# Softplus remainders summed by TensorE, and two products with their weights held: an attention and selective-scan block on one core

## The chip, the core and the metric

The kernel runs on one core of a Trainium2 chip. The engines named below are TensorE (PE; its weight loads are listed as PEld), VectorE (DVE), ScalarE (ACT), GpSimd (POOL) and SyncE (SP, which issues the DMAs). Each engine works through its own queue in order; they meet through semaphores. The metric is the device time of one execution in microseconds, as the median over several runs.

## What is computed

The input x has shape (16, 256, 32, 32): 16 batch items of 256 channels by 1024 positions. Two layers follow each other. The first is a group norm with an attention block (4 heads of 32) and a feed-forward part. The second is a group norm with a selective scan. Cut to what the change touches:

```python
ctx = sigmoid(conv(xp, gate_w) + gate_b)              # gate: 3 taps, 256 -> 256 channels
u, z = split(xs @ in_proj_w.T)                        # 512 + 512 channels
u = silu(causal depthwise conv(u))
dt, Bm, Cm = split(u @ x_proj_w.T)
delta = softplus(dt @ dt_proj_w.T + dt_proj_b)        # 512 channels x 1024 positions
A = -exp(A_log)                                       # 512 x 64
# for each position, with a state of 64 values per channel
h = exp(delta * A) * h + (delta * u) * B_t
y = sum over the 64 states of h * C_t
y = (y + u * D) * silu(z)
x = x + (y @ out_proj_w.T * ctx).reshape(B, C, H, W)  # a reshape, not a transpose
```

The last line reads a (1024 positions, 256 channels) matrix as (256, 1024) without turning it. Output channel c, position l is therefore token 4c + l // 256, channel l % 256.

## The kernel before

**The scan sets the frame.** Per batch item there are 512 channels x 64 states = 32,768 rows of 1024 positions, cut into 256 *units* of 128 rows. For unit n the main loop does, in this order:

- `load(n + 6)`: a DMA spreads two rows of delta * u (DRAM tensor `dus`) over 128 partitions into one of seven `dub` buffers; for every eighth unit a further load brings `pieces`, the rows of delta.
- `inputs(n + 4)`: POOL multiplies `dub` by B (line 956).
- one step of `outputs`: PE multiplies finished states by C into `yb` (line 998) and, once in eight units, turns the sum (line 1010); ACT copies the results out.
- `scan(n)`: DVE runs the recurrence over 128x1024 (line 973).
- `decay(n + 2)`: PE rebuilds delta from three bfloat16 pieces and spreads it over the states (line 965, into `a`), and ACT takes Exp with A as a scale per partition (line 967). There are two `a` buffers, so the matmuls for unit n + 2 wait until scan n has read its own.

All arithmetic queues keep the order in which the program was written: a chain of dependencies at the end of the kernel fixes it. The DMAs on SP are ordered by the framework's scheduler.

**Side work is a generator.** While batch item b is scanned, the kernel prepares item b + 1 (`first_norm`, `attention_layer`, `scan_inputs`) and finishes item b - 1 (`gate_and_store`). Each `yield` hands back a share of a unit, and after each unit the loop takes the next step when it is due:

```python
if at >= (1 if b + 1 < B else 8):
    due -= 1.0
    while due <= 0.0:
        due += gap(next(side, 1e9), rate)
```

A step with a share of 1 or more is never followed by another in the same unit, and `rate` stretches the shares so that all steps fit into 247 of the 256 units. A longer list of steps moves all others closer together. Item 0 is prepared alone before the first scan, and item 15 is finished alone after the last one.

**Softplus** stands at the end of `scan_inputs`. For each of the four blocks of 128 channels (`d`) and each half of 512 positions (`hf`) it computes softplus as relu(v) + log(1 + e) with e = exp(-|v|), corrected by what rounding s = 1 + e lost. Matmul (800), Abs (802), Exp (803), s (808), Relu into PSUM (809), two DVE operations for relu and the correction (813, 814), Ln (828), a DVE difference (832). Delta is then cut into three bfloat16 pieces: ACT casts (833, 842), and DVE subtracts each piece from what is left in PSUM (841, 845, the second straight into the third piece). DVE multiplies by u (837). Both halves of a block go through the steps together, about seven steps a block. PSUM tiles come from a pool of two (`mm`).

**Gate** (`gate`, line 730). The positions are the stationary operand, every fourth of them, and the weights stream through, so that the result comes out as the reshape needs it: tokens on partitions, channels along the free axis. 12 matmuls of 128x256 for each tile of 512 and two one-row matmuls for the bias (736), then Tanh (739).

**Output product** (`gate_and_store`, line 910). It has the same form: 128 tokens, every fourth, are the stationary operand, four matmuls of 128x256 are one step, eight steps make the item. Two DVE operations a tile (897, 899) multiply by the gate and add the residual, one tile behind PE.

Of the kernel before, what the change touches and what calls it, by code (L numbers as in the profile page):

```python
# [11 lines left out]
F32 = mybir.dt.float32  # L12
BF16 = mybir.dt.bfloat16
AF = mybir.ActivationFunctionType
ALU = mybir.AluOpType
# [4 lines left out]
P = 128  # L20
C = 256
KC = C // P
L = 1024
HL = 512
# [5 lines left out]
ND = DI // P  # L30
# [20 lines left out]
def attention_then_scan_kernel(  # L51
# [86 lines left out]
    def col(name, i=0, n=1):  # L138
        o, w = _COLS[name]
        assert i + n <= w  # L140
        return vec[:, o + i : o + i + n]

    gate_b = const.tile([1, C], F32, name="gate_b")
    nc.sync.dma_start(gate_b, gate_bias)
    one_row = const.tile([1, P], F32, name="one_row")
    nc.vector.memset(one_row, 1.0)
    ident = const.tile([P, P], F32, name="ident")
    make_identity(nc, ident)
    avg = const.tile([P, P], F32, name="avg")
    nc.vector.memset(avg, 1.0 / C)  # L150
    eps = const.tile([P, 1], F32, name="eps")
# [485 lines left out]
    def scan_inputs(b):  # L637
# [81 lines left out]

        gates = {}  # L720

        def gate(o, hf, q, k):
            if (hf, q, k) == (0, 0, 0):
                gates["g"] = work("g")
            if (q, k) == (0, 0):
                gates["ps"] = psum("g_ps")
            g, ps = gates["g"], gates["ps"]
            first = o * HL + hf * 2 + q
            for t in range(3):
                nc.tensor.matmul(  # L730
                    ps[:, ts(q, C)], xp[k][:, ds(first + t, P, 4)], wg_s[:, k, t, :],
                    start=(k == 0 and t == 0), stop=False,
                )
            if k < KC - 1:
                return
            nc.tensor.matmul(ps[:, ts(q, C)], one_row, gate_b, start=False, stop=True)
            if q == 1:
                table("tanh")
                nc.scalar.activation(g[:, hs(hf)], ps, AF.Tanh, scale=0.5)
                if hf == 1:  # L740
                    nc.sync.dma_start(gs[ts(o, P), :], g)

# [5 lines left out]
        for d in range(ND):  # L748
            for t in range(2):
                tap(d, t)  # L750
                if d + 1 < ND:
                    project(d + 1, t)
                yield 1
            tap(d, 2)
            table("tanh")
            nc.scalar.activation(ups[d][:, :L], us[d], AF.Tanh)
            gate(d // 2, d % 2, 0, 0)
            yield 1
            gate(d // 2, d % 2, 0, 1)
            yield 1.5  # L760
            nc.vector.scalar_tensor_tensor(us[d], ups[d][:, :L], 1.0, us[d], ALU.add, ALU.mult)
            ups[d] = None
            nc.sync.dma_start(ud[ts(d, P), :], us[d])
            gate(d // 2, d % 2, 1, 0)
            yield 1
            gate(d // 2, d % 2, 1, 1)
            yield 1.5
        gates.clear()
        del xp, body
# [25 lines left out]
        dus = dram.tile([DI, L], F32, name="dus", tag="dus")  # L795
        dpv = dps.rearrange("(k q e p x) t -> k p e q x t", k=ND, q=4, e=2, p=3)

        def begin(d, hf):
            ps = psum("d_ps")
            nc.tensor.matmul(ps, wdt4[:, ts(d, P)], dt[:, hs(hf)], start=True, stop=True)  # L800
            e = hwork("sp_e")
            nc.scalar.activation(e, ps, AF.Abs, bias=col("dt_b", d))
            nc.scalar.activation(e, e, AF.Exp, scale=-1.0)
            return ps, e

        def more(d, ps, e):
            s = hwork("sp_s")
            nc.scalar.activation(s, e, AF.Copy, bias=1.0)
            nc.scalar.activation(ps, ps, AF.Relu, bias=col("dt_b", d))
            return ps, e, s  # L810

        def rest(ps, e, s):
            nc.vector.scalar_tensor_tensor(ps, s, 1.0, ps, ALU.subtract, ALU.subtract)
            nc.vector.tensor_tensor(ps, ps, e, ALU.subtract)

        table("log")
        items = [begin(0, 0)]
        yield 1
        for d in range(ND):
            items = [more(d, *items[0]), begin(d, 1)]  # L820
            yield 1.3
            items[1] = more(d, *items[1])
            rest(*items[0])
            yield 1.1
            rest(*items[1])
            for ps, e, s in items:
                table("log")
                nc.scalar.activation(s, s, AF.Ln)
            yield 1.3
            pc = [ptp.tile([P, L], BF16, name="pc", tag="pt") for _ in range(3)]  # L830
            for hf, (ps, e, s) in enumerate(items):
                nc.vector.tensor_tensor(ps, s, ps, ALU.subtract)
                nc.scalar.copy(pc[0][:, hs(hf)], ps)
            yield 1.1
            du = work("du")
            for hf, (ps, e, s) in enumerate(items):
                nc.vector.tensor_tensor(du[:, hs(hf)], us[d][:, hs(hf)], ps, ALU.mult)
            nc.sync.dma_start(dus[ts(d, P), :], du)
            yield 1.1
            for hf, (ps, e, s) in enumerate(items):  # L840
                nc.vector.tensor_tensor(ps, ps, pc[0][:, hs(hf)], ALU.subtract)
                nc.scalar.copy(pc[1][:, hs(hf)], ps)
            yield 1.1
            for hf, (ps, e, s) in enumerate(items):
                nc.vector.tensor_tensor(pc[2][:, hs(hf)], ps, pc[1][:, hs(hf)], ALU.subtract)
            items, ps, e, s = [], None, None, None
            for p in range(3):
                for e in range(2):
                    nc.sync.dma_start(dpv[d, p, e], pc[p][e:P:2])
            if d + 1 < ND:  # L850
                items = [begin(d + 1, 0)]
            yield 1.1
        st.update(zs=zs, gs=gs, ud=ud, rows=rows, dps=dps, dus=dus)
        st["ys"] = dram.tile([DI, L], F32, name="ys", tag="ys")
        yield 1
# [18 lines left out]
    def gate_and_store(b):  # L874
        if "gate" not in state[b]:
            for go in gate_loads(b):
                go()
        ys, us, zs, gs, xs, wo_s, come = state[b].pop("gate")
        for d in range(ND):
            come.pop(0)()  # L880
            nc.vector.scalar_tensor_tensor(us[d], us[d], col("D", d), ys[d], ALU.mult, ALU.add)
            ys[d] = None
            yield 0.6
            come.pop(0)()
            nc.gpsimd.tensor_tensor(us[d], us[d], zs[d], ALU.mult)  # L885
# [7 lines left out]
        ready = []  # L893

        def finish():
            for o, hf, ps in ready:
                nc.vector.scalar_tensor_tensor(ps, gs[o][:, hs(hf)], 1.0, ps, ALU.add, ALU.mult)
# [4 lines left out]
            ready.clear()  # L902

        for o in range(KC):
            for hf in range(2):
                ps = psum3("m_ps")
                for q in range(2):
                    first = o * HL + hf * 2 + q
                    for d in range(ND):
                        nc.tensor.matmul(  # L910
                            ps[:, ts(q, C)], us[d][:, ds(first, P, 4)], wo_s[:, d, :],
                            start=(d == 0), stop=(d == ND - 1),
                        )
                    if q == 1:
                        finish()
                    if come:
                        come.pop(0)()
                    yield 1.3
                ready.append((o, hf, ps))
        finish()  # L920
        del ps
        yield 1
        state[b].clear()

# [245 lines left out]
```

## Time and profile before

| | |
|---|---|
| runs | 12599.05, 12651.92, 12653.68 us; median 12651.92 |
| the profiled execution | 12609.3 us, span 12607.5 us |
| granted TensorE clock over the span, share of full | 0.799 |
| first scan starts, last scan ends | 426.1 us, 12560.8 us |
| batch items 0 to 14 | 762 to 778 us each |
| batch item 15, with no next item to prepare | 608 us |
| DMA | 2820 MB, mean 224 GB/s |
| chain of waits, by engine | DVE 37%, PE 32%, issue 13%, ACT 8%, DMA 7%, POOL 3% |

The span is cut into the time before the first scan (item 0 is prepared), sixteen stretches of 256 units, and 47 us after the last scan. Times of single instructions below come from the one profiled execution. A group's row reads: line, engine, operation, output<-inputs, shapes, count, then busy us in total, mean ns of one, the idle time of the engine just before them, and what ended it. A float32 matmul stands in the trace as two passes, so its count is twice that of the program.

### The profile page before, as it was taken

How to read it: one execution, taken by the hardware profiler on the slowest of the kernel's cores; microseconds unless marked ns; L12 is line 12 of the kernel's file. 1: busy time of each engine (PE TensorE's matmuls, PEld its weight loads, DVE VectorE, ACT ScalarE, POOL GpSimd, SP SyncE). 2: the span in 40 equal slices, each digit the busy share in tenths (PEclk: the TensorE clock that was granted, in tenths of full speed). 3: DMA queues.
4: the chain of work that ended last, by engine and by line, in shares of the span. 5: the costliest groups of instructions: out<-in, count | busy, mean ns of one | idle time of the engine just before them, and what ended most of it. 6: DMA issues, size and time to landing. Idle time of an engine off the chain costs nothing.

```text
span 12607.5 us, 421113 instructions
## 1 busy us (share of the span) xinstructions
PE 9517.2 (75%) x184752; PEld 5493.8 (44%) x184752; DVE 11264.3 (89%) x7482; ACT 7523.0 (60%) x10758; POOL 10030.6 (80%) x4201
## 2 busy tenths in 40 slices
PE   6676876868778687786878768687686877868777
PEld 2344444444444444444444444444444444444445
DVE  2799999899999899898998999999999998989998
ACT  3565655656656565565656656565565665656554
POOL 0587878878788787887878878788887878878798
PEclk7887977878878697887878878797787978878755
DMA  1566667676676766767666676766767667676676
GB/s 53 178 224 239 220 214 239 221 244 219 216 238 227 245 216 223 240 219 245 226 223 235 220 240 221 241 219 222 237 224 247 217 223 241 221 245 217 230 250 231
DMA packets 1070137, 2819.91 MB, mean 224 GB/s; under 512 B 324162, under 2 KB 402243, under 8 KB 1068292
## 3 DMA queue, kind: packets, MB, share of 16 engines
q1 hardware_dynamic: 1068292, 2792.97, 65.0%
q8 instruction: 1444, 23.66, 0.8%
q14 instruction: 401, 3.28, 0.1%
HBM read 2513.82 MB, written 261.62 MB: 220 GB/s over the span
## 4 chain that ended last, share of the span: by engine, by line
DVE 37%; PE 32%; issue 13%; ACT 8%; DMA 7%; POOL 3%; SPq 1%; DVEq 0%; POOLq 0%; ACTq 0%
DVE h L973 27%; PE yb L998 6%; PE a L965 5%; ACT a L967 4%; DMA dub<-dus 3%; PE av L531 3%; POOL dub L956 3%; PE st_ps L543 3%; DVE over L449 2%; PE z_ps L680 2%; PE s_ps L469 2%; PE g_ps L730 2%; PE yb L1010 1%; PE m_ps L910 1%; DVE u L716 1%
## 5 line engine op out<-in xcount | busy, mean ns | idle before, releaser
L956 POOL TENSOR_TENSOR dub<-dub,bt 128x1024 f32<-128x1024 f32 x4096 | 9805.4, 2420 | 2446.0 <-DMA dub<-dus 2241.7
L973 DVE TENSOR_TENSOR_SCAN h<-a,dub 128x1024 f32<-128x1024 f32 x4096 | 9176.7, 2275 | 705.4 <-ACT a L967 406.0
L967 ACT ACTIVATE a<-a,acol 128x1024 f32<-128x1024 f32 x4096 | 4464.1, 1090 | 3157.7 <-PE a L965 3092.6
L965 PE MATMUL a<-pieces,pick 48*128 48x512 bf16 x8192 | 1914.0, 458 | 2473.6 <-DVE h L973 2362.0
L998 PEld LDWEIGHTS yb<-h,cd 128*32 128x32 f32 x131072 | 2496.9, 128 | 2639.8 <-issue 1332.2
L998 PE MATMUL yb<-h,cd 128*32 128x64 f32 x131072 | 3266.9, 252 | 342.4 <-ACT y L1004 234.8
L965 PEld LDWEIGHTS <-pick 48*128 48x128 bf16 x8192 | 597.0, 95 | 2886.7 <-issue 2256.4
L1004 ACT COPY y<-yb 128x256 f32<-128x256 f32 x2048 | 763.3, 373 | 598.5 <-PE yb L998 589.1
L531 PE MATMUL av<-pt,vv 128*64 128x512 f32 x2048 | 607.7, 674 | 2.9 <-ACT sums L520 1.6
L551 ACT ACTIVATE pt<-st_ps 128x512 f32<-128x512 f32 x1024 | 552.9, 597 | 82.9 <-PE st_ps L543 82.0
L1010 PE MATMUL yb<-turn,y 128*32 128x16 f32 x32768 | 590.1, 214 | 2.3 <-issue 1.2
L543 PE MATMUL st_ps<-sp 33*128 33x512 f32 x2048 | 583.2, 646 | 2.9 <-ACT pt L551 2.9
L1010 PEld LDWEIGHTS yb<-turn,y 128*32 128x32 f32 x32768 | 571.7, 159 | 2.6 <-ACT y L1004 1.4
L730 PE MATMUL g_ps<-w,xp 128*128 128x256 f32 x1464 | 457.0, 452 | 0.1
L1014 ACT COPY yo<-yb 128x128 f32<-128x128 f32 x512 | 135.3, 264 | 519.1 <-PE yb L1010 510.9
L730 PEld LDWEIGHTS g_ps<-w,xp 128*128 128x128 f32 x1464 | 368.7, 326 | 67.7 <-issue 58.7
L469 PE MATMUL s_ps<-kd,qm 64*128 64x512 f32 x1022 | 367.5, 617 | 14.0 <-DVE kd L444 7.5
L449 DVE CUSTOM_DVE_ANT_0 over<-s_ps,over 128x512 f32<-128x512 f32 x512 | 326.8, 676 | 24.4 <-PE s_ps L469 24.4
L910 PE MATMUL m_ps<-w,xs 128*128 128x256 f32 x1024 | 321.6, 464 | 11.4 <-POOL xs L885 11.4
L716 DVE SCALAR_TENSOR_TENSOR u<-up,cwh,u 128x1024 f32<-128x1024 f32 x192 | 302.7, 1576 | 27.9 <-ACT u L708 27.7
L477 ACT ACTIVATE over<-s_ps 128x512 f32<-128x512 f32 x511 | 275.3, 595 | 32.8 <-PE s_ps L469 32.8
L910 PEld LDWEIGHTS m_ps<-w,xs 128*128 128x128 f32 x1024 | 262.9, 328 | 59.3 <-issue 26.7
(180 smaller groups left out, 7126.8 us busy)
## 6 DMA issues: line engine op xcount, KB each, us to landing
dub<-dus SPq DMA_DIRECT2D x4096, 512.0 KB
dps<-pc SPq DMA_DIRECT2D x384, 128.0 KB
pieces<-dps SPq DMA_DIRECT2D x1024, 48.0 KB
xs<-in_x_dram SPq DMA_DIRECT2D x64, 512.0 KB
xs<-kept SPq DMA_DIRECT2D x64, 512.0 KB
zs<-z SPq DMA_DIRECT2D x64, 512.0 KB
ud<-u SPq DMA_DIRECT2D x64, 512.0 KB
dus<-du SPq DMA_DIRECT2D x64, 512.0 KB
```

What stands on the lines that cost most here:

```text
L469: nc.tensor.matmul(s, qm[c // NJ][r, c % NJ], keys[r], start=True, stop=True)
L531: nc.tensor.matmul(av[ts(e, 2 * DH)], vv[j // (NJ // 2)][:, j % (NJ // 2), 2 * pair + e, :], pts[e], start=(j == 0), stop=(j == NJ - 1),)
L543: nc.tensor.matmul(s, ka[r, ts(j, P)], qa[r, hs(hf)], start=True, stop=True)
L730: nc.tensor.matmul(ps[:, ts(q, C)], xp[k][:, ds(first + t, P, 4)], wg_s[:, k, t, :], start=(k == 0 and t == 0), stop=False,)
L910: nc.tensor.matmul(ps[:, ts(q, C)], us[d][:, ds(first, P, 4)], wo_s[:, d, :], start=(d == 0), stop=(d == ND - 1),)
L956: nc.gpsimd.tensor_tensor(v, v, blocks[units[n][0]]["bt"], ALU.mult)
L965: nc.tensor.matmul(a[:, hs(hf)], w, pieces[r], start=True, stop=True)
L967: nc.scalar.activation(a, a, AF.Exp, scale=acol[:, at : at + 1])
L973: nc.vector.tensor_tensor_scan(now["h", e][:, i, :], decays.pop(n), loaded.pop(n), 0.0, ALU.mult, ALU.add)
L998: nc.tensor.matmul(yb[ts(g, 32), ts(s, 64)], cd[:, at // 16, ts(c, 32)], hbuf[:, :, at : at + 8], start=(c == 0), stop=(c == 1),)
L1004: nc.scalar.copy(y2[:, r], yb[:, :256])
L1010: nc.tensor.matmul(some[ts(r, 32), x], y2[:, r, x:256:8], turn[:, x], start=True, stop=True)
```

## The change

Softplus becomes a generator for one half tile, with two halves in flight four steps apart:

- The relu stays in PSUM, and PE adds to it there: identity times Ln(s), and minus-identity times the correction. The correction itself is one DVE operation on SBUF tiles.
- s = e + 1 is made by POOL.
- After each bfloat16 piece PE subtracts it in PSUM with a bfloat16 minus-identity; all three pieces are casts by ACT.
- PSUM tiles come from a cycle of three banks.
- 36 steps of one unit each take the place of 29 steps with shares of 1 to 1.3. The same six piece DMAs and one `dus` DMA a block are issued as their pieces are done.

The gate holds its weights stationary and streams 512 positions, so that six matmuls make one tile, with channels on partitions; the bias moves into the Tanh. The output product holds its weights as well (four matmuls of 128x512 a step), DVE joins it with the gate into an SBUF tile, and PE turns each tile back with four matmuls of 128x128 against the identity, reading every fourth column. Three small constants are added.

```diff
+    less = const.tile([P, P], F32, name="less")
+    nc.vector.tensor_scalar(less, ident, -1.0, None, ALU.mult)
+    less_b = const.tile([P, P], BF16, name="less_b")
+    nc.vector.tensor_copy(less_b, less)
...
-            for t in range(3):
+            for at in ((0, 1), (2,), (3, 4), (5,))[part]:
+                k, t = divmod(at, 3)
                 nc.tensor.matmul(
-                    ps[:, ts(q, C)], xp[k][:, ds(first + t, P, 4)], wg_s[:, k, t, :],
-                    start=(k == 0 and t == 0), stop=False,
+                    ps, wg_s[:, k, t, ts(o, P)], xp[k][:, ds(hf * HL + t, HL)],
+                    start=(at == 0), stop=(at == 5),
                 )
-            nc.tensor.matmul(ps[:, ts(q, C)], one_row, gate_b, start=False, stop=True)
...
-        def rest(ps, e, s):
-            nc.vector.scalar_tensor_tensor(ps, s, 1.0, ps, ALU.subtract, ALU.subtract)
-            nc.vector.tensor_tensor(ps, ps, e, ALU.subtract)
...
+        def softplus(d, hf):
+            at = hs(hf)
+            ps = psum3("d_ps")
+            nc.tensor.matmul(ps, wdt4[:, ts(d, P)], dt[:, at], start=True, stop=True)
+            e = hwork("sp_e")
+            table("log")
+            nc.scalar.activation(e, ps, AF.Abs, bias=col("dt_b", d))
+            yield
+            nc.scalar.activation(e, e, AF.Exp, scale=-1.0)
+            yield
+            s = hwork("sp_s")
+            nc.gpsimd.tensor_scalar(s, e, 1.0, None, ALU.add)
+            nc.scalar.activation(ps, ps, AF.Relu, bias=col("dt_b", d))
+            yield
+            nc.vector.scalar_tensor_tensor(e, s, 1.0, e, ALU.subtract, ALU.subtract)
+            table("log")
+            nc.scalar.activation(s, s, AF.Ln)
+            yield
+            nc.tensor.matmul(ps, ident, s, start=False, stop=False, skip_group_check=True)
+            nc.tensor.matmul(ps, less, e, start=False, stop=True, skip_group_check=True)
+            del s, e
+            yield
...
+            nc.vector.tensor_tensor(du[:, at], us[d][:, at], ps, ALU.mult)
+            for p in range(3):
+                if p > 0:
+                    yield
+                    nc.tensor.matmul(
+                        ps, less_b, pc[p - 1][:, at], start=False, stop=True, skip_group_check=True
+                    )
+                nc.scalar.copy(pc[p][:, at], ps)
...
+        going = []
         for d in range(ND):
...
+            for hf in range(2):
+                going.append(softplus(d, hf))
+                for _ in range(4):
+                    for g in going:
+                        next(g)
+                    yield 1
+                if len(going) == 2:
+                    del going[0]
...
+        def project(o, k):
+            ps = psum3("m_ps")
+            for d in range(ND):
+                nc.tensor.matmul(
+                    ps, wo_s[:, d, ts(k, P)], us[d][:, hs(o)],
+                    start=(d == 0), stop=(d == ND - 1),
+                )
+            return ps
+
+        def join(o, k, ps):
+            v = gated[o, k] = hwork("v")
+            nc.vector.scalar_tensor_tensor(v, gs[k][:, hs(o)], 1.0, ps, ALU.add, ALU.mult)
+
+        def turn_back(o, hf):
+            ps = psum3("o_t")
+            for q in range(2):
+                for k in range(KC):
+                    nc.tensor.matmul(
+                        ps[:, ds(q * C + k * P, P)], gated[o, k][:, ds(hf * 2 + q, P, 4)], ident,
+                        start=True, stop=True,
+                    )
+            turned.append((o, hf, ps))
+
+        work_on = [("p", 0, 0), ("p", 0, 1), ("p", 1, 0), ("t", 0, 0), ("p", 1, 1), ("t", 0, 1), ("t", 1, 0), ("t", 1, 1)]
```

In a middle batch item the program's own order puts the eight output steps on units 17 to 24 (before: 17 to 23 and 25), attention on 78 to 126 (before: 79 to 130), the gate on 178 to 201 (184 to 207) and softplus on 209 to 244 (215 to 243).

More of the change, by code (lines that the diff above doesn't have):

```diff
@@ L141, in col @@
         return vec[:, o + i : o + i + n]
[L143 to L146, printed above, removed]
+    gate_b = const.tile([P, KC], F32, name="gate_b")
+    nc.sync.dma_start(gate_b, gate_bias.rearrange("o (k p) -> p (o k)", p=P))
+    nc.vector.tensor_scalar(gate_b, gate_b, 0.5, None, ALU.mult)
     ident = const.tile([P, P], F32, name="ident")
     make_identity(nc, ident)
+    less = const.tile([P, P], F32, name="less")
+    nc.vector.tensor_scalar(less, ident, -1.0, None, ALU.mult)
+    less_b = const.tile([P, P], BF16, name="less_b")
+    nc.vector.tensor_copy(less_b, less)
     avg = const.tile([P, P], F32, name="avg")
@@ L720, in scan_inputs, with gate @@
         gates = {}
-        def gate(o, hf, q, k):
-            if (hf, q, k) == (0, 0, 0):
+        def gate(o, hf, part):
+            if (hf, part) == (0, 0):
                 gates["g"] = work("g")
-            if (q, k) == (0, 0):
+            if part == 0:
                 gates["ps"] = psum("g_ps")
             g, ps = gates["g"], gates["ps"]
-            first = o * HL + hf * 2 + q
-            for t in range(3):
+            for at in ((0, 1), (2,), (3, 4), (5,))[part]:
+                k, t = divmod(at, 3)
                 nc.tensor.matmul(
-                    ps[:, ts(q, C)], xp[k][:, ds(first + t, P, 4)], wg_s[:, k, t, :],
-                    start=(k == 0 and t == 0), stop=False,
-                )
-            if k < KC - 1:
-                return
-            nc.tensor.matmul(ps[:, ts(q, C)], one_row, gate_b, start=False, stop=True)
-            if q == 1:
-                table("tanh")
-                nc.scalar.activation(g[:, hs(hf)], ps, AF.Tanh, scale=0.5)
+                    ps, wg_s[:, k, t, ts(o, P)], xp[k][:, ds(hf * HL + t, HL)],
+                    start=(at == 0), stop=(at == 5),
+                )
+            if part == 3:
+                nc.scalar.activation(
+                    g[:, hs(hf)], ps, AF.Tanh, scale=0.5, bias=gate_b[:, o : o + 1]
+                )
                 if hf == 1:
@@ L756, in scan_inputs @@
             nc.scalar.activation(ups[d][:, :L], us[d], AF.Tanh)
-            gate(d // 2, d % 2, 0, 0)
+            gate(d // 2, d % 2, 0)
             yield 1
-            gate(d // 2, d % 2, 0, 1)
+            gate(d // 2, d % 2, 1)
             yield 1.5
@@ L763, in scan_inputs @@
             nc.sync.dma_start(ud[ts(d, P), :], us[d])
-            gate(d // 2, d % 2, 1, 0)
+            gate(d // 2, d % 2, 2)
             yield 1
-            gate(d // 2, d % 2, 1, 1)
+            gate(d // 2, d % 2, 3)
             yield 1.5
@@ L796, in scan_inputs @@
         dpv = dps.rearrange("(k q e p x) t -> k p e q x t", k=ND, q=4, e=2, p=3)
-        def begin(d, hf):
-            ps = psum("d_ps")
-            nc.tensor.matmul(ps, wdt4[:, ts(d, P)], dt[:, hs(hf)], start=True, stop=True)
+        dus_of, parts = {}, {}
+        def softplus(d, hf):
+            at = hs(hf)
+            ps = psum3("d_ps")
+            nc.tensor.matmul(ps, wdt4[:, ts(d, P)], dt[:, at], start=True, stop=True)
             e = hwork("sp_e")
+            table("log")
             nc.scalar.activation(e, ps, AF.Abs, bias=col("dt_b", d))
+            yield
@@ L803, in begin @@
             nc.scalar.activation(e, e, AF.Exp, scale=-1.0)
-            return ps, e
-        def more(d, ps, e):
+            yield
             s = hwork("sp_s")
-            nc.scalar.activation(s, e, AF.Copy, bias=1.0)
+            nc.gpsimd.tensor_scalar(s, e, 1.0, None, ALU.add)
             nc.scalar.activation(ps, ps, AF.Relu, bias=col("dt_b", d))
-            return ps, e, s
-        def rest(ps, e, s):
-            nc.vector.scalar_tensor_tensor(ps, s, 1.0, ps, ALU.subtract, ALU.subtract)
-            nc.vector.tensor_tensor(ps, ps, e, ALU.subtract)
@@ L816, in scan_inputs @@
-        table("log")
-        items = [begin(0, 0)]
-        yield 1
-        for d in range(ND):
[L820 to L852, printed above, removed]
@@ new lines, in softplus @@
+            yield
[7 more added lines that the diff above has]
+            yield
+            if hf == 0:
+                dus_of[d] = work("du")
+                parts[d] = [ptp.tile([P, L], BF16, name="pc", tag="pt") for _ in range(3)]
@@ new lines, in softplus @@
+            du, pc = dus_of[d], parts[d]
+            nc.vector.tensor_tensor(du[:, at], us[d][:, at], ps, ALU.mult)
[6 more added lines that the diff above has]
+                nc.scalar.copy(pc[p][:, at], ps)
+                if hf == 1:
+                    if p == 0:
+                        nc.sync.dma_start(dus[ts(d, P), :], dus_of.pop(d))
+                    for e in range(2):
+                        nc.sync.dma_start(dpv[d, p, e], pc[p][e:P:2])
@@ new lines, in softplus @@
+            if hf == 1:
+                del parts[d]
+            yield
+        going = []
+        for d in range(ND):
+            for hf in range(2):
[6 more added lines that the diff above has]
+                    del going[0]
+        for _ in range(4):
+            next(going[0])
+            yield 1
+        going.clear()
@@ L892, in gate_and_store @@
             come += fetches(state[b + 2].setdefault("tok", []), state[b + 2]["kept"])
-        ready = []
+        turned, gated = [], {}
         def finish():
-            for o, hf, ps in ready:
-                nc.vector.scalar_tensor_tensor(ps, gs[o][:, hs(hf)], 1.0, ps, ALU.add, ALU.mult)
+            for o, hf, ps in turned:
                 t = xs[o][:, hs(hf)]
@@ L901, in finish @@
                     nc.sync.dma_start(out[b, ts(o, P), :], xs[o])
[L902 to L919, printed above, removed]
+            turned.clear()
+        def project(o, k):
[16 more added lines that the diff above has]
+                        start=True, stop=True,
+                    )
+            turned.append((o, hf, ps))
+        work_on = [("p", 0, 0), ("p", 0, 1), ("p", 1, 0), ("t", 0, 0), ("p", 1, 1), ("t", 0, 1), ("t", 1, 0), ("t", 1, 1)]
+        joined = []
+        for what, o, i in work_on:
+            for j in joined:
+                join(*j)
+            joined.clear()
+            finish()
+            if what == "p":
+                joined.append((o, i, project(o, i)))
+            else:
+                turn_back(o, i)
+            if come:
+                come.pop(0)()
+            yield 1.3
         finish()
-        del ps
         yield 1
```

## The prediction

> **What bounds the kernel now.** I read the page's engine totals first, then its costliest groups, then busy time by stage, then single rows.
>
> ```profile
> PE 9517.2 (75%) x184752; PEld 5493.8 (44%) x184752; DVE 11264.3 (89%) x7482; ACT 7523.0 (60%) x10758; POOL 10030.6 (80%) x4201
> ...
> L956 POOL TENSOR_TENSOR dub<-dub,bt 128x1024 f32<-128x1024 f32 x4096 | 9805.4, 2420 | 2446.0 <-DMA dub<-dus 2241.7
> L973 DVE TENSOR_TENSOR_SCAN h<-a,dub 128x1024 f32<-128x1024 f32 x4096 | 9176.7, 2275 | 705.4 <-ACT a L967 406.0
> L967 ACT ACTIVATE a<-a,acol 128x1024 f32<-128x1024 f32 x4096 | 4464.1, 1090 | 3157.7 <-PE a L965 3092.6
> ```
>
> VectorE (DVE) is busy 89%; 9177 of its 11264 us are the 4096 scans, and side work is squeezed between them. It idles only 12607.5 - 11264.3 = 1343 us. What takes an instruction off DVE therefore pays nearly in full, unless another engine then makes a scan wait. The last batch has no side preparation and shows the next floor: 608 us, POOL busy 600.
>
> Batch 4 (start 3512.8 us, 762.6 us long) by stage: output product, attention, z product, u and gate, dt/B/C product, softplus, and ten units with no side work. Columns: length, busy us (instructions) of PE, PEld, DVE, ACT, POOL, then granted clock, DMA share, GB/s.
>
> ```profile
> 3577.70:3612.60 34.90, 30.13 (x468) 23.60 (x467) 29.45 (x20) 12.54 (x16) 29.52 (x13) 0.90 0.76 269
> 3756.10:3888.00 131.90, 119.45 (x2549) 58.23 (x2548) 120.62 (x55) 107.36 (x165) 123.96 (x54) 0.99 0.70 241
> 4009.80:4038.60 28.80, 28.31 (x405) 13.26 (x405) 24.89 (x19) 17.78 (x24) 21.68 (x11) 0.89 0.67 218
> 4038.60:4125.00 86.40, 74.63 (x1244) 50.01 (x1243) 84.70 (x49) 49.07 (x67) 76.74 (x29) 0.96 0.61 211
> 4125.00:4144.20 19.20, 17.95 (x306) 9.66 (x305) 15.54 (x8) 10.87 (x15) 13.85 (x7) 0.91 0.63 210
> 4144.20:4245.70 101.50, 60.43 (x1353) 35.30 (x1356) 95.80 (x80) 70.27 (x108) 72.37 (x32) 0.66 0.69 227
> 4245.70:4267.60 21.90, 16.38 (x391) 10.77 (x382) 21.88 (x11) 12.37 (x16) 13.92 (x6) 0.50 0.60 204
> ```
>
> Length less DVE busy is what DVE lost: 5.5 us in the output product, 11.3 in attention, 1.7 in the gate stage, 5.7 in softplus. So softplus is DVE's stage and PE is spare there, at a clock of 0.66; in the output product and attention PE is as full as DVE. A bare unit costs 21.9/10 = 2.19 us.
>
> **The change, part by part.** *Softplus, DVE.* These rows are what each half tile costs now:
>
> ```profile
> L813 DVE SCALAR_TENSOR_TENSOR d_ps<-sp_s,d_ps 128x512 f32<-128x512 f32 x127 | 87.4, 688 | 59.5 <-ACT d_ps L809 59.4
> L814 DVE TENSOR_TENSOR d_ps<-d_ps,sp_e 128x512 f32<-128x512 f32 x127 | 88.8, 699 | 4.4
> L832 DVE TENSOR_TENSOR d_ps<-sp_s,d_ps 128x512 f32<-128x512 f32 x127 | 80.7, 680 | 0.8 <-ACT pc L833 0.7
> L841 DVE TENSOR_TENSOR d_ps<-d_ps,pc 128x512 f32<-128x512 f32 x127 | 81.0, 683 | 0.7 <-ACT pc L842 0.7
> L845 DVE TENSOR_TENSOR pc<-d_ps,pc 128x512 bf16<-128x512 f32 x127 | 80.2, 672 | 1.5 <-DMA dps<-pc 0.8 <-ACT pc L842 0.7
> L800 PE MATMUL d_ps<-dt,wdt 128*128 128x512 f32 x254 | 202.3, 892 | 32.9 <-DVE pc L845 21.2 <-ACT d_ps L809 11.7
> ```
>
> All five DVE operations go (0.688+0.699+0.680+0.683+0.672 = 3.42 us); the product with u stays. One comes: (s-1)-e with every operand in SBUF. No such row of this size exists: the same operation reading PSUM takes 0.668 (L670), and half of the 128x1024 SBUF rows 0.79 (L716) to 0.98 (L881). I take 0.79, the in-place one. Net 2.63 us a half, 8 halves: 21.1 us a batch, 316 us over the 15 batches that run beside scans.
>
> *Softplus, what the other queues get.* Per half PE gains identity times s and minus-identity times e (float32, two passes each) and two bfloat16 products; ACT swaps the copy L808 (0.628) for a third cast (0.591); POOL gains s = e + 1. For that I bound 0.44 (an eighth of the 128x4096 memset, 3.51) to 1.18 (half of L956), taking 0.9. DMAs are the same in number and still trail the scans' loads, six units ahead. The steps now come one per unit, four units per half: 36 units against 30, the rest of the batch moving some six units earlier.
>
> In steady state four units need DVE 4 x 2.19 + 0.79 + 0.67 = 10.2 us; POOL 4 x 2.36 + 0.9 = 10.3; ACT 4 x 1.09 + 0.9 of y copies + seven operations of 4.4 = 9.7. Nothing is left spare, so waits decide. The worst unit holds the finish of one half and the start of the next: six float32 passes in a row on PE. Behind them in PE's queue stand the y products of the scan output (0.65 to 1.1) and the decay matmuls (0.4 to 0.6), then ACT's Exp of 1.09, for which a scan waits, since only two decay tiles exist. A pass takes 0.43 at full clock and 0.85 to 1.0 at half, as here (two passes, 2.07):
>
> ```profile
> 4939.75 2.07 PE L800 MATMUL d_ps<-dt,wdt 128*128 128x512 f32 x2
> ```
>
> I walk the queues from the end of a scan. Full clock: decay 0.65, six passes to 3.3, y products to 4.05, next decay, Exp 4.65 to 5.75, scan at 5.8; but DVE, after its scan (2.2), waits for the sums (2.5), multiplies, scans from 3.2 to 5.4: 0.3 + 0.4 lost. Later in the cycle ACT runs cast, Relu, cast and Ln behind the Exps, so that the next sums start 0.45 late: about 1.2 us lost per half. Half clock for the first four passes: sums at 4.3, scan from 5.0, next Exp not before 6.5, the following scan at 7.65: 2.1 + 0.4 lost, and 0.3 from Ln: 2.8. The trace's own cold case is milder: the same walk for the second of two neighbouring d_ps units gives 1.4 lost, and I count 0.5 there. The clock rises and falls here:
>
> ```profile
> 4162.00:4176.00 14.00, 8.74 (x141) 4.76 (x140) 13.48 (x13) 8.26 (x13) 9.39 (x5) 0.50 0.56 193
> 4176.00:4184.00 8.00, 5.36 (x168) 3.18 (x168) 7.97 (x6) 6.87 (x11) 2.62 (x2) 0.93 0.89 260
> 4184.00:4200.00 16.00, 8.81 (x150) 4.89 (x152) 15.97 (x15) 9.19 (x14) 15.26 (x7) 0.50 0.64 208
> ```
>
> Two d_ps units near 4171 to 4177 raise it for about 8 us, then it drops. Blocks will come every 11 to 13 us, so about half their passes run slow: 1.9 us per half, 8 x 1.9 + 2 to start and drain - 5.7 lost now = +11.5 us a batch (bounds 8 x 1.2 and 8 x 2.8: +5.9 to +18.7).
>
> [...]
>
> *Gate.* Twelve float32 matmuls of 256 columns (0.30 a pass, both passes 0.60) and two bias matmuls (0.64) become six of 512 (0.86): 8.5 us less 5.2, four times a batch, 13 us of PE. It lies beside DVE, which lost 1.7 us in 86.4: I count -0.5 (0 to -1.5).
>
> *Output.* 32 matmuls of 256 columns (0.60 each, 19 us) become 16 of 512 (0.86) and 16 of 128 with a strided weight load (bounds 0.32, the 128-column row L505, to 0.60): 19 to 23 us; DVE keeps eight operations of 0.68. PE is full here and the products come bunched, three units in a row, and the joining operation makes DVE wait for the product just issued: +2 (bounds -1 to +5).
>
> *Attention* loses about three of its 53 units, and PE must do the same in fewer: +2 (0, if DVE set the pace, to 6.6, three units of 2.19).
>
> Sum a batch: -21.1 + 11.5 - 0.5 + 2 + 2 = -6.1, times 15 = -92 us. Outside the scans: the first softplus runs alone, 372 to 424 us; there each half is one chain (six cold passes 5.5, Abs, Exp, add, DVE, Ln 3.8): 8 x 8.5 against 52, I take +15 (bounds -10 to +30); last output product +2. Together -75. The profiled run was 12609.3 (span 12607.5), so 12534; the median of the runs is 12651.9, 43 above it, so I forecast **12577**, a ratio of 0.994. A few tenths of a per cent is the runs' own spread; within 0.5% (63 us) counts as no change.
>
> **Rivals.** *The clock stays up.* Bounds 1.2 a half: -21.1 + 5.9 + 3.5 = -11.7, times 15, + 17 = -158: 12490; were POOL's 10.3 per cycle the only floor left (0.1 above DVE), another 8 x 1.1 x 15 = -132: 12360. For: one stage earlier, PE at the same fullness ran at 0.89 to 0.96. Against: three of four units are thin. *TensorE takes DVE's place: slower.* Each block of six passes at half clock, all cold (6 x 1.0), holds the decay behind it: by the same walk the next Exp ends at 9.5 where the scan could have begun at 5.1. 4.0 lost per half gives -21.1 + 28.3 + 3.5 = +10.7 a batch, + 177 in all: 12830. It decides from 2.5 us per half on (8 x 2.5 + 2 - 5.7 + 3.5 + 1.1 = 21). For: 0.50 to 0.66 now, POOL's add queued behind a scan product and before the DVE step. Against: 0.5 counted where a walk gave 1.4. *Nothing gained*: the gain is just spent at 2.4 per half: 12650.
>
> **Chances and range.** Forecast 0.45 (own range 12480 to 12650), clock stays up 0.15, slower 0.28, nothing gained 0.12. Faster by over 0.5%: 0.33 of the first and the 0.15: 0.48; within: 0.20; slower: 0.32, with part of the last. Range 12390 to 12790.
>
> **What would show it.** DVE busy per batch down by 21 us (700.8 to 680); softplus DVE idle near 17 to 20 us, ended by "PE d_ps" at the product with u and by "ACT a" at the scan; clock there above 0.66; gate PE busy down 13. I am wrong if softplus idle stays under 10 (gain of 1% or more) or exceeds 26, or if output or attention lose over 5 more each.

## The result, and the profile after

The changed kernel takes **13027.06 us** (median of 4 runs, 12988.2 to 13030.82) against 12632.26 us (12599.05 to 12653.68) for the kernel before, measured beside it: a ratio of **1.0316**, 95% interval 1.0286 to 1.0347. It is 3% slower; 12577 was forecast. The profiled execution took 12988.2 us (span 12986.1, granted clock 0.826), 378.6 us more span than before.

The engine totals and costliest groups of the changed kernel, as on its page (columns as before; in the first line the time, the share of the span, and the instructions):

```profile
PE 9735.3 (75%) x184496; PEld 5218.5 (40%) x184496; DVE 11234.5 (87%) x6972; ACT 7491.3 (58%) x10758; POOL 10253.0 (79%) x4329
...
L997 DVE TENSOR_TENSOR_SCAN h<-a,dub 128x1024 f32<-128x1024 f32 x4096 | 9170.8, 2273 | 770.8 <-ACT a L991 413.8
...
L812 POOL TENSOR_SCALAR sp_s<-sp_e 128x512 f32<-128x512 f32 x128 | 190.7, 1490 | 766.8 <-ACT sp_e L809 766.8
...
L815 DVE SCALAR_TENSOR_TENSOR sp_e<-sp_s,sp_e 128x512 f32<-128x512 f32 x128 | 343.4, 2683 | 68.0 <-POOL sp_s L812 68.0
...
L827 DVE TENSOR_TENSOR du<-u,d_ps 128x512 f32<-128x512 f32 x127 | 87.2, 687 | 278.8 <-PE d_ps L820 260.6
```

DVE has 510 instructions fewer and is busy for the same time: 11234.5 us against 11264.3. The forecast had it 316 lower. The one DVE operation that the change adds, L815, stands there with a mean of 2.68 us; the forecast priced it at 0.79. And the product with u (L827) now waits for TensorE's sums, 261 us in all.

Batch 4 by stage (start 3569.5 us here, 795.3 us long; columns as in the prediction: length, busy us and instructions of PE, PEld, DVE, ACT, POOL, then clock, DMA share, GB/s): output product, attention, u and gate, dt/B/C product, softplus; the row of the z product is left out.

```profile
3635.10:3671.00 35.90, 35.23 (x436) 21.31 (x435) 25.26 (x18) 11.33 (x14) 23.66 (x11) 0.90 0.62 212
3806.60:3950.90 144.30, 132.20 (x2640) 66.23 (x2640) 125.43 (x60) 111.86 (x172) 129.16 (x57) 0.94 0.67 227
...
4097.70:4184.70 87.00, 72.33 (x1250) 35.81 (x1249) 83.13 (x49) 49.97 (x68) 72.38 (x28) 0.92 0.59 203
4184.70:4200.90 16.20, 14.37 (x236) 6.74 (x235) 15.48 (x9) 11.06 (x15) 11.65 (x6) 1.00 0.79 269
4200.90:4333.50 132.60, 88.80 (x1644) 44.69 (x1644) 107.83 (x54) 76.30 (x116) 102.90 (x47) 0.83 0.56 195
```

Softplus went from 101.5 us on 30 units to 132.6 on 36. Six bare units (units with no side work, 2.19 us each before) are 13.1, so 18 us of it are loss. The output product loses a few us more (DVE was idle for 10.6 of its 35.9). TensorE's granted clock in softplus was higher (0.83 against 0.66), and the stage was longer all the same.

The same cut at scan starts, as means over batch items 2 to 13, worked out from each run's trace: length, DVE time of side work, DVE idle, in us per item. Side work is summed instruction by instruction, and instructions overlap their neighbours a little, so that scans, side work and idle time add up to more than the length. Lengths compare only over equal numbers of units: output is cut over ten units in the kernel before and nine elsewhere, group norm over twelve. The runs besides the two kernels are described below; "36 units" is the kernel before with softplus given as many units as the change uses.

| us per item | item | softplus | output | attention (56 units; before: 58) | group norm of the second layer |
|---|---|---|---|---|---|
| before | 768.6 / 151.3 / 65.1 | 101.7 / 32.7 / 5.9 (30 units) | 32.5 / 5.5 / 5.2 | 147.8 | 40.9 |
| before, 36 units (run 5) | 767.7 / 148.9 / 66.7 | 115.0 / 32.7 / 6.0 | 30.7 / 5.5 / 5.5 | 141.9 | 39.9 |
| after | 796.0 / 148.2 / 92.3 | 132.0 / 28.0 / 24.2 | 35.8 / 5.5 / 10.5 | 144.9 | 43.6 |
| PSUM operand (run 3) | 780.1 / 134.8 / 89.7 | 115.2 / 11.1 / 24.3 | | | |
| after, shares of run 5 (run 12) | 791.0 / 146.9 / 88.5 | 130.9 / 28.0 / 23.2 | 35.8 / 5.5 / 10.5 | 141.8 | 39.9 |
| fastest version (run 11) | 760.8 / 129.8 / 75.8 | 103.2 / 11.0 / 13.1 | 30.8 / 5.5 / 5.6 | 141.6 | 39.9 |

So, set on equal units, softplus lost 132.0 - 115.0 = 17.0 us an item: side work fell by 4.7 where 21.1 was forecast, and idle time rose by 18.2. The rest of the 28.3 us by which an item is longer than in run 5 (796.0 against 767.7) lies mainly in other stages: 5.1 in output, 3.0 in attention, 3.7 in the group norm.

**One operation, two durations.** L815 over the whole run, as minimum/median/maximum in ns:

```profile
L815 DVE SCALAR_TENSOR_TENSOR sp_e<-sp_s,sp_e x128: 691/2829/2841, 336.7 to 12272.6; 128x512 f32<-128x512 f32 x128
```

The first softplus is prepared before any scan runs. The changed kernel's DVE timeline in the second half of it (start, duration in us, then the instruction, then the idle time before it and what ended it):

```profile
376.65 0.69 DVE L815 SCALAR_TENSOR_TENSOR sp_e<-sp_s,sp_e 128x512 f32<-128x512 f32 x1 [3.71 <-POOL sp_s L812]
...
386.61 0.69 DVE L815 SCALAR_TENSOR_TENSOR sp_e<-sp_s,sp_e 128x512 f32<-128x512 f32 x1 [4.05 <-POOL sp_s L812]
...
397.58 0.69 DVE L815 SCALAR_TENSOR_TENSOR sp_e<-sp_s,sp_e 128x512 f32<-128x512 f32 x1 [2.75 <-POOL sp_s L812]
...
407.34 2.82 DVE L815 SCALAR_TENSOR_TENSOR sp_e<-sp_s,sp_e 128x512 f32<-128x512 f32 x1 [3.75 <-POOL sp_s L812]
```

Alone it takes 0.69 us. The last of these takes 2.82, and it is the first that meets a POOL product: L980's first one, `dub` times B, starts at 407.3. Beside the scans that is the rule, as in a stretch of batch item 5, cut from the timeline of all engines:

```profile
5028.61 1.49 POOL L812 TENSOR_SCALAR sp_s<-sp_e 128x512 f32<-128x512 f32 x1 [3.38 <-ACT sp_e L809]
...
5030.07 9.70 POOL L980 TENSOR_TENSOR dub<-dub,bt 128x1024 f32<-128x1024 f32 x4
5030.14 2.83 DVE L815 SCALAR_TENSOR_TENSOR sp_e<-sp_s,sp_e 128x512 f32<-128x512 f32 x1 [0.27 <-POOL sp_s L812]
...
5035.76 2.07 PE L819 MATMUL d_ps<-sp_s,ident 128*128 128x512 f32 x2
...
5037.62 1.54 PE L820 MATMUL d_ps<-sp_e,less 128*128 128x512 f32 x2
...
5039.00 1.02 PE L804 MATMUL d_ps<-dt,wdt 128*128 128x512 f32 x2
...
5039.20 0.69 DVE L827 TENSOR_TENSOR du<-u,d_ps 128x512 f32<-128x512 f32 x1 [1.86 <-PE d_ps L820]
```

POOL's add ends, and that end releases L815. The same end lets POOL begin its next product, 5030.07, just before DVE's 5030.14. That product takes 2.34 us, until 5032.41; L815 ends at 5032.97, 0.56 later. It spent most of its time waiting for the product, while DVE counted as busy. The whole trace says the same: the 7 of the 128 that started while POOL ran nothing took 0.69 us, and the other 121 started 0.06 to 0.50 us into a POOL product, and each ended 0.55 us after that product did. POOL pays as well: its next product takes 2.79 us here (5032.37 to 5035.16), as after nearly all of the 121, where the median of all products is 2.36. Later the block of six passes on TensorE starts, the first three at half clock (1.0 each; the granted clock was 0.51 from 5035.7 to 5038.7), and the product with u waits 1.86 us for it.

### The profile page after: what moved, and what is told of

Its sections match the earlier page's. It is cut to its first block, busy times and chain, and to the rows that moved or that the text cites. A ratio compares the mean times of both kernels' runs of the same rounds, so it can differ in the third digit from the quotient of the medians.

```text
span 12986.1 us, 419930 instructions
## 1 busy us (share of the span) xinstructions
PE 9735.3 (75%) x184496; PEld 5218.5 (40%) x184496; DVE 11234.5 (87%) x6972; ACT 7491.3 (58%) x10758; POOL 10253.0 (79%) x4329
## 4 chain that ended last, share of the span: by engine, by line
DVE 32%; PE 28%; issue 18%; DMA 8%; POOL 7%; ACT 6%; SPq 1%; DVEq 0%; POOLq 0%; ACTq 0%
DVE h L997 23%; POOL dub L980 7%; DMA dub<-dus 4%; PE yb L1022 4%; PE a L989 4%; ACT a L991 4%; PE av L534 3%; PE st_ps L546 3%; DVE over L452 2%; PE m_ps L911 2%; PE z_ps L683 2%; PE s_ps L472 2%; DMA xs<-ud 1%; DVE u L719 1%; PE yb L1034 1%
## 5 line engine op out<-in xcount | busy, mean ns | idle before, releaser
L980 POOL TENSOR_TENSOR dub<-dub,bt 128x1024 f32<-128x1024 f32 x4096 | 9842.2, 2426 | 1821.1 <-DMA dub<-dus 1702.8
L989 PE MATMUL a<-pieces,pick 48*128 48x512 bf16 x8192 | 1842.5, 441 | 2650.1 <-DVE h L997 2531.1
L1022 PEld LDWEIGHTS yb<-h,cd 128*32 128x32 f32 x131072 | 2384.2, 124 | 2724.7 <-issue 1535.9
L1022 PE MATMUL yb<-h,cd 128*32 128x64 f32 x131072 | 3126.4, 245 | 278.3 <-ACT y L1028 182.9
L812 POOL TENSOR_SCALAR sp_s<-sp_e 128x512 f32<-128x512 f32 x128 | 190.7, 1490 | 766.8 <-ACT sp_e L809 766.8
L733 PE MATMUL g_ps<-xp,w 128*128 128x512 f32 x732 | 416.1, 682 | 0.0
L815 DVE SCALAR_TENSOR_TENSOR sp_e<-sp_s,sp_e 128x512 f32<-128x512 f32 x128 | 343.4, 2683 | 68.0 <-POOL sp_s L812 68.0
L807 ACT ACTIVATE sp_e<-d_ps,vec 128x512 f32<-128x512 f32 x127 | 87.3, 688 | 433.2 <-PE d_ps L804 433.0
L827 DVE TENSOR_TENSOR du<-u,d_ps 128x512 f32<-128x512 f32 x127 | 87.2, 687 | 278.8 <-PE d_ps L820 260.6
L719 DVE SCALAR_TENSOR_TENSOR u<-up,cwh,u 128x1024 f32<-128x1024 f32 x192 | 269.7, 1405 | 27.2 <-ACT u L711 26.9
```

What stands on the lines that cost most here:

```text
L980: nc.gpsimd.tensor_tensor(v, v, blocks[units[n][0]]["bt"], ALU.mult)
L989: nc.tensor.matmul(a[:, hs(hf)], w, pieces[r], start=True, stop=True)
L1022: nc.tensor.matmul(yb[ts(g, 32), ts(s, 64)], cd[:, at // 16, ts(c, 32)], hbuf[:, :, at : at + 8], start=(c == 0), stop=(c == 1),)
```

## Experiments

Twelve further kernels were run. The theory after reading the trace was that L815 collides with POOL's products; the rivals were that TensorE's block sets the pace, that the longer list of steps crowds the other stages, and that the gate or the output product costs the time.

**1. Which part: softplus alone.** The softplus of the change with the gate and output product of before.

> Softplus as in the changed kernel; gate and output product as before. If the loss lies in softplus (its stage is 132 us long per batch item in the changed kernel, 102 before), this stays near 12940 us, a ratio of 1.02 to 1.03 to the kernel before. If the bunched output products were the larger part, it falls to 1.01 or less.

Measured 13027.6 us, ratio 1.0338 (1.0322 to 1.0353). The whole loss comes with the new softplus, though not all of it in its own stage: against run 5 an item is 29.3 us longer, 17.3 of it in softplus, 2.7 in attention, 4.2 in the group norm and 3.8 in the stages from the z product to the dt/B/C product.

**2. Gate and output product alone**, with the softplus of before.

> Gate and output product as in the changed kernel; softplus as before. By the idle time of VectorE in the output stage (10.5 us per batch item against 5.2) I expect about 5 us per item, 15 items: 12710 us, 1.006. If moving work onto TensorE were harmless there, 1.000; if the products were the larger part of the loss, 1.015 or more.

Measured 12603.11 us, ratio 1.0001 (0.999 to 1.0012). The expected loss did not come. DVE does wait more in the output product (139 us in all for `m_ps` at the join, against 14 before; the stage takes 37.1 us an item against 32.5, both over ten units), but the item is only 1.1 us longer (769.7 against 768.6): the u and gate stage gives back 2.7 (83.6 against 86.3), the stage behind it 1.3.

**3. Move the correction into PSUM.** The DVE operation reads PSUM and one SBUF tile in place of two SBUF tiles, and TensorE adds e. Everything else is the changed kernel.

```diff
-            nc.vector.scalar_tensor_tensor(e, s, 1.0, e, ALU.subtract, ALU.subtract)
+            nc.vector.scalar_tensor_tensor(ps, ps, 1.0, s, ALU.add, ALU.subtract)
...
-            nc.tensor.matmul(ps, less, e, start=False, stop=True, skip_group_check=True)
+            nc.tensor.matmul(ps, ident, e, start=False, stop=True, skip_group_check=True)
```

> The changed kernel, but the correction step of VectorE takes one operand from PSUM: relu + 1 - s is formed in place in PSUM, and TensorE adds e with the identity in place of subtracting the correction. Same number of operations on every engine. Theory of the collision (an operation with both operands in SBUF waits until GpSimd's running product ends): the step falls from 2.68 to 0.69 us, 2 us x 8 halves x 15 items = 240 us less, 12760 to 12800 us. Rival, that TensorE's six passes set the pace of the softplus stage: the saved time turns into a longer wait for PE, and the total stays within 60 us of 13027.

Measured 12758.7 us, ratio 1.012 (1.0105 to 1.0135): 268 us less than the changed kernel. The group of this operation in that run:

```profile
L815 DVE SCALAR_TENSOR_TENSOR d_ps<-d_ps,sp_s 128x512 f32<-128x512 f32 x127 | 88.8, 700 | 137.4 <-ACT d_ps L813 109.8 <-POOL sp_s L812 15.2 <-ACT pc L834 11.3
```

The same engine, the same shape, at the same place in the program: 0.70 us in place of 2.68. Its release changed a little: the add ended only 15 us of its waits, and ACT's Relu, which now comes last, 110. But POOL's products still run: of the 120 beside scans, 118 started during one, and all took 0.67 to 0.70 us. The group fell from 343.4 to 88.8 us, 255 of the 268. This settles the largest cause.

**4. Keep both operands in SBUF, but let ACT make s**, so that the release no longer falls on the start of a POOL product.

```diff
-            nc.gpsimd.tensor_scalar(s, e, 1.0, None, ALU.add)
+            nc.scalar.activation(s, e, AF.Copy, bias=1.0)
```

> The changed kernel, but s = e + 1 is made by ScalarE, as before the change; the correction step still reads two SBUF operands. If GpSimd's own addition (1.49 us, and 0.77 ms of waiting for Exp in all) is the cause, the time falls by 200 us or more. If the collision with GpSimd's products is, the step still waits, though no longer every time at the very start of a product: a mean of 1.5 to 2.4 us, and 12900 to 13000 us.

Measured 12845.6 us, ratio 1.0186 (1.0156 to 1.0217), 181 us less than the changed kernel. That lies between the two times that were expected, so the time alone does not choose. The group does:

```profile
L815 DVE SCALAR_TENSOR_TENSOR sp_e<-sp_s,sp_e 128x512 f32<-128x512 f32 x128 | 163.6, 1278 | 135.9 <-ACT sp_s L812 135.9
```

It fell by 180 of the 181 us, the mean from 2.68 to 1.28 us with the same operands. Beside the scans 45 of them started while POOL ran nothing and took 0.67 to 0.69 us; 75 started during a product, with a median of 1.64, and ended 0.55 to 0.64 us after that product. So for this operation the collision needs two things: two SBUF operands (run 3 took 0.70 us beside running products without them), and a start while a POOL product runs (0.69 us at most without one). The release by POOL's own add made it nearly certain, in 121 of 128.

**5. Is the longer list of steps itself the loss?** The kernel before with seven empty steps of one unit behind softplus.

```diff
+        for _ in range(7):
+            yield 1
```

> The kernel before with seven empty steps of one unit each after softplus, so that all other steps move closer together as far as in the changed kernel; no work is added or taken. If the crowding itself costs (VectorE idle in attention, output and feed-forward grew by 1.5, 5 and 4 us per item where softplus was changed), 3 to 6 us per item: 12650 to 12690 us, 1.004 to 1.007. If crowding is free, 1.000.

Measured 12591.51 us, ratio 0.9989 (0.9971 to 1.0006). The crowding has no net cost. It also moved the other stages to other units, and the second group norm became 1 us an item shorter; see run 11.

**6 to 8. Spread the block of passes.** With the correction in PSUM, half the sum no longer depends on Ln. Run 6 moves the product of identity and e one unit ahead (below, against run 3; the product with Ln(s) then ends the sum); run 7 also moves Relu to follow Abs, so that the DVE step need not wait for it; run 8 is run 7 with the gate and output product of before.

```diff
             nc.vector.scalar_tensor_tensor(ps, ps, 1.0, s, ALU.add, ALU.subtract)
+            nc.tensor.matmul(ps, ident, e, start=False, stop=False, skip_group_check=True)
...
-            nc.tensor.matmul(ps, ident, e, start=False, stop=True, skip_group_check=True)
```

> The kernel with the PSUM operand, with TensorE's product for e issued one unit earlier, right behind the correction step, so that four float32 passes stand in a row and not six. If that block is what VectorE waits for at the product with u (1.3 us a half now, ended by PE), that wait falls below 0.5 us: 8 x 15 x 0.8 = 100 us less, 12650 to 12690 us. Rival, that the decay's own round trip over TensorE and ScalarE sets the pace: unchanged within 30 us of 12759.

> As the one before, with Relu issued right after Abs, two units earlier, so that the correction step no longer waits for ScalarE (1.07 us a half with the PSUM operand). Expected 80 to 130 us below it, 12540 to 12600 us; if Relu only delays the decay's Exp instead, no change against it.

> All three edits to softplus, with the gate and the output product as before the change. Since gate and output product moved the time by nothing against the kernel before, equal to the previous run within 0.5%; if the bunched output products cost in this denser order, 40 to 80 us less.

Measured 12720.56 (1.0087, 1.0055 to 1.0118), 12755.31 (1.0127, 1.0098 to 1.0157) and 12751.14 us (1.0119, 1.009 to 1.0148). Spreading the sum brought 38 us, less than expected, and freeing Relu cost 35 where 80 to 130 had been expected as gain. Run 8's waits (who waited for whom, us in total, times, longest) show why:

```profile
POOL dub L964 <- DMA dub<-dus: 1809.7, 1550, 8.5
...
DVE d_ps L818 <- POOL sp_s L816: 223.6, 108, 8.1
```

With Relu gone as the last to arrive, DVE waited for POOL's add, up to 8.1 us, and the add stands in POOL's queue behind products that wait for their loads, up to 8.5 us. Runs 9 and 10 test this.

**9 and 10. Take the add off POOL as well.** Run 9 is run 7 with s made by ACT (the edit of run 4); run 10 has the gate and output product of before besides.

> PSUM operand, e's product one unit earlier, Relu behind Abs, and s = e + 1 on ScalarE in place of GpSimd. In the three runs without this VectorE waited 224 us in all for GpSimd's addition, which stands in GpSimd's queue behind products that wait for a DMA (up to 8.1 us). If that is what is left, about 200 us less than 12755: 12540 to 12580 us, level with the kernel before or just below it. Rival, that ScalarE is then the engine VectorE waits for: no gain, 12700 or more.

> The same with the gate and output product as before the change: within 0.3% of the run beside it, since this pair alone moved nothing; the output stage should idle 5 us less per item and some other stage more.

Measured 12644.34 (1.0029, 1.0015 to 1.0043) and 12623.35 us (1.0016, 1.0002 to 1.0031): 111 and 128 us less than runs 7 and 8. A time level with that of before, or just below it, had been expected; run 10 came within 0.2% of it and neither came below. In run 9 softplus itself had become good: 105.6 us on 36 units against 115.0 for the old form. The loss had to lie in stages that nobody had touched: attention at 145.3 us against 141.9 in run 5, the second group norm at 43.9 against 39.9.

**11 and 12. Put the untouched stages where run 5 had them.** The loop stretches all shares by one rate, which follows from their sum. With the shares of the change it is 1.2294, in run 5 it was 1.2345. A share of 1.3 for one softplus step in four restores 1.2345, and run 11's steps up to unit 208 then stand on the same units as in run 5. Run 11 does this to run 10, run 12 to the changed kernel.

```diff
-                for _ in range(4):
+                for step in range(4):
...
-                    yield 1
+                    yield 1.3 if step == 2 else 1
```

> The previous kernel (three edits to softplus, addition on ScalarE, gate and output as before) with a share of 1.3 for one softplus step in four, so that every other step stands on the same unit as in the kernel with empty steps. Softplus itself now takes 105.5 us per item against 115.0 there in the same 36 units, but attention, group norm and the u stage, whose code is the same, took 4, 4 and 4.6 us more. If their place among the units is the cause, they return to 142, 40 and 86 us: 10 to 13 us per item, 12430 to 12480 us, 0.988 to 0.991. If something else that softplus leaves behind (the banks of PSUM, GpSimd's lag) is, no change: 12600 to 12630.

> The changed kernel with the same shares alone. If the place of the untouched steps cost it some 8 us per item as well, 12880 to 12930 us; if not, 13027 within 30.

Measured **12467.81 us**, ratio **0.9881** (0.9863 to 0.99), for run 11, and 12943.62 us, 1.0267 (1.0247 to 1.0287), for run 12. The one edit is worth 156 us in the first and 83 in the second; by the ratios, each to the kernel before measured beside it, about 170 and 62. Part of the mechanism shows in the adds of the second group norm, whose operands are all in SBUF. First the changed kernel, then run 12: duration in ns as minimum/median/maximum.

```profile
L660 DVE TENSOR_TENSOR xp<-xp,xs x32: 1202/3152/3375, 261.8 to 12022.4; 128x1024 f32<-128x1024 f32 x32
```

```profile
L660 DVE TENSOR_TENSOR xp<-xp,xs x32: 1193/1216/2794, 273.3 to 11982.8; 128x1024 f32<-128x1024 f32 x32
```

In the changed kernel 27 of the 32 took over 1.5 us, in run 12 only 12 did, and these for less long, and each of these started while a POOL instruction ran; the group's busy time went from 86.8 to 51.8 us. Attention gave another 3.1 us an item; why it is quicker there was not tried. The kernel before stood badly too (82.5 us for this group), so most of this is time that was to be had, rather than time that the change took.

Run 11 is the fastest version found. Its page and its softplus in batch 4:

```profile
PE 9644.7 (77%) x185520; PEld 5482.7 (44%) x185520; DVE 10951.6 (88%) x6972; ACT 7537.8 (60%) x10886; POOL 10002.0 (80%) x4201
```

```profile
4083.30:4185.90 102.60, 81.53 (x1639) 40.80 (x1632) 90.16 (x53) 79.66 (x124) 83.38 (x37) 0.85 0.77 248
```

DVE is busy for 313 us less than in the kernel before. Side work in softplus is 11.0 us an item against 32.7, 21.7 less, where the forecast had promised 21.1. In batch 4 DVE loses 12.4 us in this stage; the old form lost 5.7 on six units fewer. Whether the new gate and output product would do better or worse in this arrangement was not tried.

## Why the prediction was wrong

**The step that failed: "(s-1)-e with every operand in SBUF ... I take 0.79, the in-place one."** It measured 2.68 us on average. The side work of softplus fell by 4.7 us an item where 21.1 was forecast: 16.4 x 15 = 246 us, against 255 that run 3 took out of this one group. The prediction's sign for it, DVE busy per batch down by 21 us, failed: 703.5 us an item before, 703.7 after. The nearest rows held the warning, but I read their means and halved them. The row that I used, and one that I removed, as minimum/median/maximum in the kernel before:

```profile
L716 DVE SCALAR_TENSOR_TENSOR u<-up,cwh,u x192: 1251/1260/3445, 316.5 to 11792.3; 128x1024 f32<-128x1024 f32 x192
```

```profile
L814 DVE TENSOR_TENSOR d_ps<-d_ps,sp_e x127: 698/699/700, 377.8 to 11911.3; 128x512 f32<-128x512 f32 x127
```

The first is a mixture: 1.26 us for most, up to 3.45 for some, and the difference of 2.19 is nearly a POOL product (median 2.36). The 41 of them over 1.5 us each ended 1.08 to 1.09 us after a POOL product, as those of L815 end 0.55 after one: the wait reached 2.19 us on 128x1024 and 2.15 on 128x512 (2.84 less 0.69), so halving it with the tile was wrong. The second has an operand in PSUM, and takes 0.70 every time, though 58 of its 128 started while a POOL instruction ran. The right bounds would have been 0.63 and 0.63 + 2.3 = 2.9, and the upper one decides: POOL releases the operation at the moment when it starts its next product.

Side by side: 0.69 us alone, 2.83 behind a product of 2.34, and 0.70 with an operand in PSUM, also for the 118 of run 3 that started during a product. Why only the form with two SBUF operands waits, the runs do not show.

**Softplus idle, "+11.5 a batch".** It was +18.2 on equal units (24.2 against 6.0), just under the upper bound of +18.7. The mechanism was as described: the product with u ends its waits on "PE d_ps", 260.6 us in 124 waits, 2.1 each, the number of the half-clock walk. That the collision does not make this idle time is shown by run 3, where it is gone and the idle time is 24.3. Only half of the passes were to run slow. In the trace the median pass of both sums (L819, L820) is 1.06 us, and of the dt product behind them (L804) 0.73. The granted clock was 0.50 at the start of 216 of the 256 passes of L819, of 247 of L820 and of 142 of L804: most blocks start at half clock, and some reach the full clock at their end. Each of the three as minimum/median/maximum in ns:

```profile
L819 PE MATMUL d_ps<-sp_s,ident x254: 927/1061/1222, 347.6 to 12278.8; 128*128 128x512 f32 x127
...
L820 PE MATMUL d_ps<-sp_e,less x254: 593/1061/1061, 349.4 to 12280.5; 128*128 128x512 f32 x127
...
L804 PE MATMUL d_ps<-dt,wdt x254: 592/732/1061, 341.6 to 12266.6; 128*128 128x512 f32 x127
```

By 8 x lost + 2 the 24.2 us are 2.8 per half, the bound with half clock for the first four passes. How much of it the slow passes alone cost stays open: runs 9 to 11 brought the idle time to 15.5, 15.3 and 13.1 with the median pass of the first sum at 0.94 to 1.06 us still. The mean clock of 0.83 in the stage said nothing about the passes that were waited for, so "clock there above 0.66" came true and proved nothing.

Two smaller things belong to softplus. POOL's add takes 1.49 us, above the upper bound of 1.18, which rested on a memset and a product of other shapes. And DVE's rows overlap their neighbours a little: taken singly they add up to 11752 us before, where the page's busy time is 11264, and after to 11659, where it is 11235. The overlap fell by 63 us, so that removed operations are worth somewhat less than the sum of their durations. Softplus on equal units was forecast at -21.1 + 11.5 = -9.6 us an item and gave +17.0. Of the 26.6 between, L815 is 16.4 and idle time 6.7; the other 3.5 are overlap lost in this stage (63 us over 16 items is 3.9).

**Output "+2 (-1 to +5)".** The stage's DVE idle rose by 5.3 us, just over the bound. But run 2 shows that next to nothing of it reached the end when the gate went with it. **Gate:** -0.5 was forecast; run 2 gave 2.7 less for its stage. TensorE's busy time for it fell by 8.4 us an item, not 13, since a new pass kept TensorE busy for 0.57 us (416.1 us over 732 passes) and not 0.43.

**Attention, "+2" for crowding.** Run 5: nothing, net. What the sum did not hold at all is that moving stages by a unit makes them longer or shorter, 83 us in run 12; for the adds of the group norm that is the same collision (the 27 long ones of the changed kernel each ended 1.08 to 1.09 us after the POOL product they met), for attention the cause stays open. **Outside the scans:** the first softplus was to cost +15, at most +30. From its first dt product to the first scan it took 87.2 us against 55.3, +32. The scans nevertheless began 6.4 us earlier (419.7 against 426.1), by luck: the z product, which the change does not touch, began at 267 us against 296, and over the runs of this case that start lay anywhere between 267 and 307. Why it varies stays open. The tail after the last scan grew by 10 us (46.7 to 56.8), not 2.

**The rivals.** "TensorE takes DVE's place" ended on the right side, but its price of 4.0 per half was not reached: 2.8 were lost. "Nothing gained" is what run 3 shows within softplus, 115.2 us against 115.0 on equal units: with the collision gone, the saved DVE time came back as idle time. No rival named the collision, and even the slowest of them, 12830, with 0.79 for that operation, fell short of the time.

## What to carry to other kernels

Price an added VectorE operation by where its operands lie, and read minimum, median and maximum of the nearest rows, not their mean: a maximum that lies about one GpSimd instruction above the minimum (3.45 against 1.25 us in L716, with products of 2.36) pointed to a wait here, and that wait did not shrink with the tile (2.19 us on 128x1024, 2.15 on 128x512). If GpSimd is busy nearly always (79% of the span here), try such an operation with an operand in PSUM (0.70 us in place of 2.68 in run 3), or at least let another engine release it (1.28 in run 4). Before an idea is given up as too slow, look at whether the untouched stages got slower: here the shares alone decided between 12623 and 12468 us.

## What was not expected of the hardware

- The blocked DVE instruction counts as busy in the trace: L815 shows 2.83 us of work and 0.27 of idle time, though 0.69 is its own.
- Placement by single units moved whole stages: with nothing else changed, the same adds of the second group norm had a median of 3.15 or 1.22 us.
- A GpSimd add of a constant over 128x512 took 1.49 us, where its product of two tiles over 128x1024, four times the reads, took 2.34.
